# Twenty rows per ky in place of nineteen in the sampling products of a two-layer convolution kernel, with one x hat tile

## The chip, the cores and the metric

The kernel runs on one core of a Trainium2 chip. The metric is device time in microseconds, from the start to the end of one execution. TensorE is called PE here, VectorE DVE, ScalarE ACT, GpSimd POOL, and SyncE, which only issues DMAs, SP. All arithmetic is in fp32.

## What is computed

The input x holds 32 images of 128 channels and 32 by 32 pixels. Layer 0 adds to x a state space convolution over the 1024 pixels of the normalised image, 1024 channels wide, followed by a gated linear unit, a layer norm and a projection back to 128 channels. Layer 1 adds a deformable depthwise convolution of the normalised image. Its core is this loop over 64 taps (8 by 8), in which each tap samples the image at a shifted, fractional place:

```python
px = gx[None] + koff_t[0] + off_t[..., 0]
py = gy[None] + koff_t[1] + off_t[..., 1]
ix = px * sx - 0.5
iy = py * sy - 0.5
...
s = ((1 - dx) * (1 - dy))[:, None] * gather(y0i, x0i) + (dx * (1 - dy))[:, None] * gather(y0i, x0i + 1) + ((1 - dx) * dy)[:, None] * gather(y0i + 1, x0i) + (dx * dy)[:, None] * gather(y0i + 1, x0i + 1)
return (acc + s * w_t[None, :, None, None], None)
```

The offsets `off_t` come from a 3 by 3 depthwise convolution of the same image. They are small, so that all samples of one output row lie within a window of 8 by 8 pixels.

## The kernel before

`ssm_kernel_table` and `ssm_convolution` compute the state space convolution of all images and write it to HBM (`y_d`). They end near 1.5 ms and the change does not touch them. Then `main_block` does two things for each image, and interleaves them.

`first_part(b)` is the gated unit, norm and projection of image b. For each half image (512 pixels) and each of 8 groups of output channels it runs 8 matmuls for the gate (`gpg`, L808), 8 for the value (`gpv`, L831) and one for h (`gph`, L847), each 128 by 128 by 512. Between them DVE, ACT and POOL make the gate's sigmoid, the products, squares and sums. The result goes to `x1_d`.

`second_part(b)` is the deformable convolution of image b. It samples by matmul. An image column position u (0 to 38) is the output column plus the tap's kx, and v (1 to 37) is the output row plus the tap's ky. For each of 17 groups of u ("packs") there is a tile `ds` of 128 partitions by 16 slots by `CELLS` words. A slot is one (u, kx); its `CELLS` = 8 · `NV` words are 8 runs, one for each ky, of `NV` rows v. The partitions are two sides of 64: each side holds the weights of an 8 by 8 pixel window, and the sides divide the rows v. Side 0 starts at row `VBASE[0]`, side 1 at row `VBASE[1]`. Most packs have all 16 slots, two have 14, two 13 and one 8 (m in the code).

How a pack's `ds` comes about:

- `prepare(b)` computes the offsets of an image step by step during the second part of the image before. It lays them out by (u, ky, v): `spread` (L984) copies rows of `NV` words from HBM to HBM, `gather` (L999) loads them into a tile of 128 by `HSUB` words, and eight `hat` steps (L1010 and L1011 on ACT, L1012 the store from ACT's queue) make the weights in x, max(0, 1 − |offset − k|), for k = 0 to 7, each in a tile `dh` of the pool `hatpool`, and store them to HBM (`dhat`).
- `load_x` (L1110, on SP's queue) loads a pack's x weights from there into `ds`, and `load_y` (L1125) the plain offsets in y into `dhy`, in two halves.
- `hat_y` (L1145, L1146) makes the y weights of `dhy` on ACT in four parts, and `weights` (L1151) multiplies them into `ds` on DVE, in four parts per pack.

How it is used: a pack's rows are cut in four pieces (`blocks_of`). Piece 0 has the border rows, in runs of 6, 4, 2 and 1; pieces 1 to 3 have 4 rows each for all eight ky, and read them in two windows of 2 rows. The matmul (`dps`, L1227) has 64 rows of image pixels (`dxw`) as stationary operand, and as moving operand it reads `ds` at

```python
frm = s[half, 0, ky * NV + v0 - VBASE[side] + r0 :]
...
[CELLS, m],
[step * NV + skew, rows], [1, r1 - r0],
```

So a matmul of pieces 1 to 3 reads m slots times 8 ky times a pair of adjacent words. The two sides' matmuls are issued in turn. Pieces 0 and 1 form one block, pieces 2 and 3 another, and each piece and side has a PSUM bank, four in all. DVE multiplies what the block left in PSUM with the taps' weights into `prod` (L1243), which frees the banks; POOL adds up the eight ky (L1269) and adds to the accumulator (L1275). There are two `ds` tiles, three `dhy` tiles and, before the change, two `dh` tiles.

What sets the order: it is written out by hand. `run_along` takes pieces of `first_part(b + 2)` and `second_part(b)` in turn, so that both progress at the same share of a planned cost, and every engine has one queue in that order. The steps of `prepare(b + 1)` are issued at fixed places (`due`) in the second part of image b. In the opening, image 0 is prepared beside the first part of image 1; at the end, the second parts of the last two images run with nothing beside them.

Of the kernel before, what the change touches and what calls it, by code (L numbers as in the profile page):

```python
# [512 lines left out]


NU = W + 7
NV = 19
VBASE = (1, 19)
CELLS = 8 * NV
PIECES = 4
SIDE = NU * 8 * CELLS  # L520
# [69 lines left out]
def main_block(nc, tc, const, ins, x, u_d, y_d, x1_d, out, offmax):  # L590
# [18 lines left out]
    SB, HB = 2, 3  # L609
    KS = 16 * H  # L610
    ctx = ExitStack()
    with ctx:

        def pool(name, bufs, space=None):
            kw = {} if space is None else {"space": space}
            return ctx.enter_context(tc.tile_pool(name=name, bufs=bufs, **kw))

        one, two = pool("mb1", 1), pool("mb2", 2)
        spool, hypool, hatpool = pool("mbs", SB), pool("mbh", HB), pool("mbq", 2)
        ypool = pool("mby", YB)  # L620
        tpool = pool("mbt", 5)
        dram = pool("mb_dram", 2, DRAM)
# [84 lines left out]
        def at(t, offset, ap):  # L707
            return bass.AP(tensor=t.tensor, offset=t.offset + offset, ap=ap)
# [175 lines left out]
        def prepare(b):  # L884
# [97 lines left out]
            def spread(a, side):  # L982
                def run():
                    nc.sync.dma_start(  # L984
                        at(
                            rel_d[b % 2], a * NCOL + side * SIDE,
                            [[NV, 64], [8 * CELLS, NU], [1, NV]],
                        ),
                        at(
                            rel_n[b % 2], a * ASTEP + LEAST - 7 * H + VBASE[side],  # L990
                            [[KSTEP - 1, 64], [H, NU], [1, NV]],
                        ),
# [178 lines left out]
        def second_part(b, steps):  # L1171
# [6 lines left out]
            for n in range(NP):  # L1178
# [9 lines left out]
                for i in range(0, PIECES, 2):  # L1188
# [10 lines left out]
                    for piece in (i, i + 1):  # L1199
# [7 lines left out]
                        for parts in zip(blocks_of(0, piece), blocks_of(1, piece)):  # L1207
# [6 lines left out]
                            for part in range(len(parts[0][1])):  # L1214
                                for side in range(2):
                                    (ky, _, v0, _, step, skew), wins = parts[side]
                                    w, r0, r1 = wins[part]
                                    half = slice(64 * side, 64 * side + 64)
                                    frm = s[half, 0, ky * NV + v0 - VBASE[side] + r0 :]
                                    frm = bass.AP(  # L1220
                                        tensor=frm.tensor, offset=frm.offset,
                                        ap=[
                                            frm.ap[0], [CELLS, m],
                                            [step * NV + skew, rows], [1, r1 - r0],
                                        ],
# [139 lines left out]
@with_exitstack  # L1365
def kernel(ctx: ExitStack, tc: tile.TileContext, ins, out):
    nc = tc.nc
    x = ins["x"]
    cpool = ctx.enter_context(tc.tile_pool(name="const", bufs=1))
    dram = ctx.enter_context(tc.tile_pool(name="scratch", bufs=1, space=DRAM))  # L1370

    const = {}
    for name in ("gavg", "davg"):
        const[name] = cpool.tile([P, P], F32, tag=name, name=name)
        nc.sync.dma_start(const[name], ins[name])
    const["eps"] = cpool.tile([P, 1], F32, tag="eps", name="eps")
    nc.vector.memset(const["eps"], 1e-5)
    const["one"] = cpool.tile([P, 1], F32, tag="one", name="one")
    nc.vector.memset(const["one"], 1.0)
    offmax = cpool.tile([P, B], F32, tag="offmax", name="offmax")  # L1380

    kp_d = dram.tile([D, KPW], F32, tag="kp_d", name="kp_d")
    u_d = dram.tile([B, C, L], F32, tag="u_d", name="u_d")
    y_d = dram.tile([D, B, NJ, P], F32, tag="y_d", name="y_d")
    x1_d = dram.tile([B, C, L], F32, tag="x1_d", name="x1_d")

    ssm_kernel_table(nc, tc, ins, kp_d)
    ssm_convolution(nc, tc, const, ins, x, u_d, kp_d, y_d)
    main_block(nc, tc, const, ins, x, u_d, y_d, x1_d, out, offmax)
    deformable_redo(nc, tc, const, ins, x1_d, out, offmax)  # L1390
# [85 lines left out]
```

## Time and profile before

| | |
|---|---|
| Median of 3 runs | 12964.31 us (12957.98 to 12971.92) |
| The profiled execution | 13042.8 us, of which the span from the first to the last instruction is 13041.0 us |
| Busy in the span: PE, DVE, ACT, POOL | 12345.9, 8228.4, 5368.1, 8027.5 us |
| Sampling matmuls `dps`, L1227 | 23936 records, 2860.9 us busy |
| Weights `ds`, L1151 | 2176 instructions on DVE, mean 1317 ns |
| x hats, L1010 and L1011 | 256 each on ACT, 899 and 915 ns (median) |
| Opening of the deformable part, first `dps` | at 1849 us |

The profile is of one execution, and the other times are of executions without a profile. A row of the groups gives the line, engine and operation, what it writes and reads with the shape, the count, the busy time, the mean of one, and the engine's idle time just before with what ended it. PE's means overlap, because matmuls are pipelined: the distance between the starts of two records is what one costs.

### The profile page before, as it was taken

The numbers are of one execution on the slowest core, as the hardware profiler recorded it, in microseconds if no ns is written. First come the engines' busy times: TensorE is split into PE (matmuls) and PEld (weight loads), VectorE is DVE, ScalarE is ACT, GpSimd is POOL, SyncE is SP. The second block draws the span as 40 slices with busy tenths as digits, with TensorE's granted clock in tenths as the row PEclk, the third lists the DMA queues.
The fourth block names the chain that finished last, engine by engine and source line by source line (L and its number), as shares of the span: only waits on it lengthen the run. The fifth ranks groups of instructions, "written<-read, shape, count | busy, mean of one in ns | idle before, by whom it ended". The sixth has DMA issues, their size and how long they took to land.

```text
span 13041.0 us, 157419 instructions
## 1 busy us (share of the span) xinstructions
PE 12345.9 (95%) x51362; PEld 6725.6 (52%) x51362; DVE 8228.4 (63%) x14315; ACT 5368.1 (41%) x7823; POOL 8027.5 (62%) x6987
## 2 busy tenths in 40 slices
PE   7999999999999999999999999999999999999965
PEld 7999444444444444444444444444444444444444
DVE  5555136666666666666666666666666666666667
ACT  4443124444444444444444444444444444444443
POOL 2555126666666666666666666666666666666668
PEclk9999999999999999999999999999999999999976
DMA  7898146666676666666666676666666666676676
GB/s 237 268 278 275 49 101 169 171 169 165 176 173 171 166 166 163 178 169 169 172 165 171 169 176 167 170 166 164 174 174 166 174 165 171 170 171 174 163 174 176
DMA packets 1521916, 2276.56 MB, mean 175 GB/s; under 512 B 619586, under 2 KB 835266, under 8 KB 1520066
## 3 DMA queue, kind: packets, MB, share of 16 engines
q1 hardware_dynamic: 1382210, 1959.47, 60.7%
q10 hardware_dynamic: 89728, 172.65, 3.6%
q0 software_dynamic: 49152, 134.28, 3.4%
q8 instruction: 413, 6.77, 0.2%
q14 instruction: 413, 3.38, 0.1%
HBM read 1948.11 MB, written 400.64 MB: 180 GB/s over the span
## 4 chain that ended last, share of the span: by engine, by line
PE 85%; DMA 7%; SPq 3%; DVE 2%; issue 1%; ACT 1%; POOL 0%; ACTq 0%; DVEq 0%; POOLq 0%
PE gpv L831 26%; PE gpg L808 25%; PE dps L1227 18%; PE psy L320 5%; PE gpo L736 3%; PE psz L237 3%; PE gph L847 3%; DMA ds<-dhat 3%; DMA dhy<-rel_d 2%; DVE ds L1151 1%; SPq L1125 1%; SPq L984 1%; DVE prod L1243 1%; SPq L1110 1%; PE gpm L758 0%
## 5 line engine op out<-in xcount | busy, mean ns | idle before, releaser
L1269 POOL TENSOR_TENSOR prod<-prod 128x512 f32<-128x512 f32 (+3 forms) x3808 | 4939.0, 1329 | 1741.0 <-DVE prod L1243 1698.4
L1243 DVE TENSOR_TENSOR prod<-dps,k_weight_slots 128x512 f32<-128x512 f32 (+16 forms) x8704 | 3121.3, 406 | 1520.8 <-PE dps L1227 1327.5
L808 PE MATMUL gpg<-gy,g_w_glu 128*128 128x512 f32 x8192 | 3827.9, 610 | 130.8 <-DMA gy<-y_d 111.2
L831 PE MATMUL gpv<-gy,g_w_glu 128*128 128x512 f32 x8192 | 3743.1, 599 | 0.0
L1151 DVE TENSOR_TENSOR ds<-ds,dhy 128x608 f32<-128x608 f32 (+2 forms) x2176 | 2766.0, 1317 | 807.7 <-DMA ds<-dhat 563.6
L1227 PE MATMUL dps<-ds,dxw 64*128 64x128 f32 (+14 forms) x23936 | 2860.9, 383 | 417.3 <-DVE prod L1243 411.2
L1227 PEld LDWEIGHTS dps<-ds,dxw 64*128 64x128 f32 x23936 | 2015.6, 199 | 1553.6 <-DVE prod L1243 636.0
L808 PEld LDWEIGHTS gpg<-gy,g_w_glu 128*128 128x128 f32 x8192 | 1535.0, 193 | 2095.2 <-issue 1910.4
L831 PEld LDWEIGHTS gpv<-gy,g_w_glu 128*128 128x128 f32 x8192 | 1510.8, 190 | 1886.0 <-issue 1886.0
L869 POOL TENSOR_TENSOR gs<-gs,gq 128x512 f32<-128x512 f32 x448 | 642.8, 1435 | 2468.7 <-ACT gq L868 2468.7
L1145 ACT ACTIVATE dhy<-dhy,k_minus_y 128x608 f32<-128x608 f32 (+2 forms) x2176 | 1645.6, 756 | 795.8 <-DMA dhy<-rel_d 481.3
L1146 ACT ACTIVATE dhy<-dhy,one 128x608 f32<-128x608 f32 (+2 forms) x2176 | 1672.2, 768 | 70.7
L868 ACT ACTIVATE gq<-gr 128x512 f32<-128x512 f32 x448 | 280.7, 627 | 2514.4 <-DVE gr L860 2513.2
L839 DVE SCALAR_TENSOR_TENSOR gs<-gpv,k_b_glu,gs 128x512 f32<-128x512 f32 x512 | 383.9, 750 | 1430.9 <-PE gpv L831 1407.4
L815 ACT ACTIVATE gs<-gpg,k_b_glu 128x512 f32<-128x512 f32 x512 | 352.0, 688 | 1955.0 <-PE gpg L808 1938.5
L1275 POOL TENSOR_TENSOR dacc<-dacc,prod 128x256 f32<-128x256 f32 (+6 forms) x1184 | 1048.2, 885 | 92.8
L357 POOL DMA_DIRECT2D y_d<-yo x1024 | 590.0, 583 | 692.8 <-ACT yo L344 633.2
L320 PE MATMUL psy<-toe,z 128*128 128x192 f32 x4096 | 668.3, 326 | 7.6 <-DVE z L242 5.5
L320 PEld LDWEIGHTS psy<-toe,z 128*128 128x128 f32 x4096 | 663.4, 196 | 11.7 <-DVE z L242 6.8
L738 POOL TENSOR_TENSOR gs<-gs,gr 128x512 f32<-128x512 f32 x448 | 644.7, 1439 | 0.0
L335 DVE TENSOR_TENSOR psy<-psy,t 128x256 f32<-128x256 f32 (+2 forms) x768 | 333.8, 435 | 346.4 <-ACT t L328 329.6
L847 PE MATMUL gph<-gu,k_W_enc 128*128 128x512 f32 x1024 | 522.9, 592 | 0.0
(164 smaller groups left out, 6037.5 us busy)
## 6 DMA issues: line engine op xcount, KB each, us to landing
dhy<-rel_d SPq DMA_DIRECT2D x3264, 152.0 KB
ds<-dhat SPq DMA_DIRECT2D x832, 380.0 KB
ds<-dhat SPq DMA_DIRECT2D x448, 456.0 KB
dxw<-dxw_d SPq DMA_DIRECT2D x832, 224.0 KB
y_d<-yo POOLq DMA_DIRECT2D x1024, 128.0 KB, 4.2
gy<-y_d SPq DMA_DIRECT2D x512, 256.0 KB
u<-u_d SPq DMA_DIRECT2D x224, 512.0 KB
dhat<-dh ACTq DMA_DIRECT2D x256, 370.5 KB
```

Of the source, the lines that this page charges most:

```text
L320: nc.tensor.matmul(ps[:, c // 2, c % 2, :], rows[i][:, (g * CG + c0 + c) // 2, c % 2, :], toe[:, c0 + c, :], start=True, stop=True,)
L738: nc.gpsimd.tensor_add(sums[0], sums[0], r)
L808: nc.tensor.matmul(gate, w_glu[:, k, D + m * P : D + m * P + P], ys[k], start=(k == 0), stop=(k == KD - 1),)
L831: nc.tensor.matmul(val, w_glu[:, k, m * P : m * P + P], ys[k], start=(k == 0), stop=(k == KD - 1),)
L847: nc.tensor.matmul(h, w_enc[:, m * P : (m + 1) * P], u, start=True, stop=True)
L1145: nc.scalar.activation(t, t, AF.Abs, bias=minus_y)
L1146: nc.scalar.activation(t, t, AF.Relu, scale=-1.0, bias=const["one"])
L1151: nc.vector.tensor_mul(s_of[h][:, cut], s_of[h][:, cut], t)
L1227: nc.tensor.matmul(to[side][:, :, :, r0:r1], xw[half, w, :], frm, start=True, stop=True,)
L1243: nc.vector.tensor_mul(bass.AP(tensor=at_y.tensor, offset=at_y.offset, ap=[at_y.ap[0], [H, m], [step * (KS - 1) + skew, rows], [1, run],], ...
L1269: nc.gpsimd.tensor_add(row(to), row(to), row(frm))
L1275: nc.gpsimd.tensor_add(to, to, total[:, slot * H : (slot + nj) * H].rearrange("p (s y) -> p s y", y=H),)
```

## The change

`NV` becomes 20 and side 1 begins at row 18. So a run of one ky has 20 words, a slot 160 in place of 152, side 0 holds rows 1 to 20 and side 1 rows 18 to 37; the word at which a run begins, ky · NV + v0 − VBASE + r0, is even for every run of two or more words. `CELLS`, `SIDE`, `NCOL` and `HSUB` follow: a hat tile is 780 words wide in place of 741, a `ds` tile 2560 words in place of 2432. The pool of the hat tiles has one buffer in place of two. The number of instructions and DMAs and their order on each engine stay.

```diff
 NU = W + 7
-NV = 19
-VBASE = (1, 19)
+NV = 20
+VBASE = (1, 18)
 CELLS = 8 * NV
...
-        spool, hypool, hatpool = pool("mbs", SB), pool("mbh", HB), pool("mbq", 2)
+        spool, hypool, hatpool = pool("mbs", SB), pool("mbh", HB), pool("mbq", 1)
```

## The prediction

> **What bounds the kernel now.** I read the page first: which engine is busy, and for how long of the span.
>
> ```profile
> span 13041.0 us, 157419 instructions
> PE 12345.9 (95%) x51362; PEld 6725.6 (52%) x51362; DVE 8228.4 (63%) x14315; ACT 5368.1 (41%) x7823; POOL 8027.5 (62%) x6987
> ```
>
> Then the same split into stretches: the second is where 30 of the 32 images have both parts of the work side by side, the third is the end, where the deformable part (`second_part`) runs alone.
>
> ```profile
> 1850.00:12500.00 10650.00, 10362.79 (x40317) 5108.42 (x40314) 7015.96 (x12089) 4511.66 (x6179) 6945.60 (x5569) 0.98 0.68 169
> 12500.00:13041.00 541.00, 278.45 (x1515) 214.59 (x1514) 391.39 (x707) 224.22 (x298) 407.18 (x330) 0.63 0.71 179
> ```
>
> The order in a row is PE, PEld, DVE, ACT, POOL, clock, DMA share, GB/s. In the long stretch PE is busy 97%, DVE and POOL 66 and 65%. In the last it is busy half the time.
>
> Third, what PE still waits for, between 3000 and 12500 us:
>
> ```profile
> PE dps L1227 <- DVE prod L1243: 169.0, 53, 7.6
> PE gpg L808 <- DMA gy<-y_d: 87.5, 27, 5.6
> ```
>
> That is 257 us in 9500. So a nanosecond taken off PE's own stream in this stretch is worth nearly a nanosecond, as long as DVE follows.
>
> Last, how PE's time is made up, from the chain of waits and the groups by shape:
>
> ```profile
> 6004.55 3.43 PE gpg L808 x8
> 6018.48 2.38 PE dps L1227 x16
> L808 PE MATMUL gpg<-gy,g_w_glu 128*128 128x512 f32 x8192 | 3827.9, 610 | 130.8 <-DMA gy<-y_d 111.2 <-ACT gs L815 19.7
> L1227 PE MATMUL dps<-ds,dxw 64*128 64x256 f32 x9216 | 1562.5, 459 | 22.2 <-DVE prod L1243 18.0 <-ACT gn_r L914 3.4 <-ACT dvt L1032 0.7
> ```
>
> Each fp32 matmul leaves two records. The mean ns overlap, so I use pitches, the distance between starts. Eight 512-column records take 3.43 us: 429 ns each, 0.838 ns per column. The sampling block `dps` has 16 records of 256 columns. Its two sides, on partitions 0-63 and 64-127, start within 10 ns of each other, so this is eight pairs in 2.38 us. The start times of the single records give 273 ns from pair to pair inside the block, plus some 100 ns once at each end. At 0.838 ns a column, 256 columns would be 215 ns. **The sampling matmuls stream 27% slower per column than the GLU ones.** This gap is what the change is about.
>
> The records of different size (m slots, median pitch over the steady part) show where it comes from. Pair runs (rows read two words at a time): m=16: 274, 14: 242, 13: 225, 8: 139; that is 16.9 ns a slot, where 16 columns should take 13.4: 3.5 too much. The border piece's runs of six: 191, 167, 155, 12.0 a slot where 12 columns should take 10.1: 1.9 too much. Runs of four: 119, 105, 98, hardly too much. With 19 rows, a run begins at word 19·ky + constant, so half the pairs begin at an odd word and every fourth straddles a 16-byte line (two of eight ky). The line model: a slot's 8 pairs touch 10 lines; 16.9/10 is 1.7 ns a line. The odd run of six touches lines as 1+4+1, and 1.9 too much is again about two near-empty visits at 1.7 in place of two words at 0.84 (2·1.7 − 1.7). The odd run of four, 1+3, loses little, as seen.
>
> [...]
>
> **The change, part by part.**
>
> 1. *Even starts (PE, L1227).* With 20 rows ky·20 is even and a multiple of 4; starts become 6, 8 (side 0: v0=7, base 1) and 2, 4 (side 1: v0=20, base 18), the border runs 0, 42, 84 and 134, 94, 54. All even; no pair straddles a line, as the ds tiles begin on multiples of 32 bytes in both builds. The instruction order on PE is identical. New pitches: columns × 0.838 + 3.6 (the present fit's constant): m=16: 218, 14: 191, 13: 178, 8: 112 [...]. The line model gives the same for m=16: 128 lines × 1.7 = 218. Gain per pitch 56, 51, 47, 27 ns. Twelve pair pitches a pack (3 pieces × 2 windows × 2 records), packs per image 12, 2, 2, 1 of these sizes: 12·(12·56 + 2·51 + 2·47 + 27) = 10.7 us. Runs of six, two pitches a pack: 12·2·27 + 2·2·23 + 2·2·21 = 0.8. Runs of four, down to 111: 12·15 = 0.2. Together **11.8 us per image**, of a period of 355. On the path for 30 images: −353. Bounds: 60 ns a pitch if no constant stays (−380); nothing if reading is not the cause.
>
> 2. *Longer rows on DVE (L1151).* Four multiplies a pack grow by 5.3%: per image 54 of 608 to 640, 10 of 456 to 480, 4 of 304 to 320, 2032 elements. From the fastest 304 (460 ns) and 608 (773): 1.03 ns each, 2.1 us an image. DVE has a third of its time free: not on the path by itself.
>
> 3. *Longer rows on ACT.* Two activations of dhy per part: 0.84 ns an element (532 and 785 ns at 304 and 608), 3.4 us an image; hats 741 to 780, 16 × 33 ns = 0.5 us. ACT is 42% busy: nothing.
>
> 4. *More bytes.* ds and dhy loads, hats and rel all grow by 1/19. Issues times KB: ds 632, dhy 632, dhat 97, rel 36 MB, so +74 MB of 2277, DMA share .68 to about .72 with the shorter time. The number of issues on SP, ACT and POOL stays. A ds load comes out in the chain at 6 to 8 us, so each takes 0.3 to 0.4 us more. DVE already waits for them (451.6 us, 135 times in the steady part), and behind that wait in DVE's order stand the products that free PSUM for PE. The half pack in which they must land shrinks by 0.4 too. So DVE's ds are up to 0.8 us later per pack where they are late now, four or five packs an image, and a third of DVE's lateness reaches PE today (169 of 452). 5·0.8/3 is 1.3; I take 1.5 us an image: **+45**. Ends: 0, and 4 us an image (+120) if more packs turn late.
>
> 5. *One hat tile (L1010).* Each Abs now waits until the previous hat's store has left the tile; behind it on ACT stand sigmoids, squares and dhy. In steady images the next Abs comes 8.9 to 19 us after the previous issue (in the last set of hats 2 and 7 us, twice); its packets are gone after 4.5 us (median), 7.0 (nine in ten), 8.9 at most. Nothing, except single cases. In the opening (1787 to 1809 us) eight hats follow at 2.7 us each and the packets need 2.3 after issue: 1.9 + 2.3 = 4.2 us each, seven times 1.5, and PE is waiting for a sigmoid behind them (19.7 us in this place): **+10** (8 to 25).
>
> 6. *The end.* The last two images run alone; their chain is ds loads and ds multiplies, and PE at a lowered clock is too slow to be hurt by reading. 34 packs × (0.3 load, part of it hidden, + 0.13) : **+12** (0 to 25).
>
> Sum: −353 + 45 + 10 + 12 = **−286**. The profiled execution took 13042.8 us, its span 13041.0; that is 0.6% above the median 12964.31. 12757/13042.8 times the median: **12680**.
>
> **The rivals.**
>
> *Rival 1: half of it returns as DVE's lateness.* For: 20% of the packs' first blocks begin before the last products of the previous pack are done, and the median slack there is 1.6 us. Against: DVE's place is tied to PE's own results (gate, value and h groups in between), so it moves with PE. If each half pack loses 0.17 us of its 0.35, −150 net: about 12815.
>
> *Rival 2 (slower): PSUM writing, not reading, sets the pair pitch.* Place: L1227, where a window writes two of each four words. Price: pitch stays at 272-274, no gain; parts 4 to 6 cost about 1 us an image + 10 + 12, +52: 13016. Decides if pair pitches stay above some 268 ns (6 ns are worth what the costs are). Against: runs of six write without gaps and are slow too.
>
> *Rival 3: the hats stall ACT in every image.* From a landing later than the 8.9 us gap on: 2 us at each second hat, 8 us an image on ACT, perhaps half on PE: −353 + 120 + 67, about 12800. Packets' times speak against.
>
> *That the change doesn't act:* were the tile to begin at an odd word, all pairs would be odd; the addresses exclude it.
>
> **How the numbers follow.** Main case 0.70, rival 1 0.16, rival 2 0.09, rival 3 0.05. The main case's own ends are −380 + 8 = −372 (12594) and −353 + 120 + 25 + 25 = −183 (12782); reaching over rival 1 and 3 gives 12590 to 12840. A measurement can tell about 0.2%, 26 us. Faster: main, rivals 1 and 3 nearly whole, 0.88; same 0.03 (rival 2 with part of the gain); slower 0.09.
>
> **What would show it.** Right: L1227 64x256 mean from 459 to about 400 ns, x16 blocks of 1.95 us in the chain in place of 2.38, image period 346 us in place of 355, GLU records unchanged at 429. Wrong: blocks at 2.38 (rival 2); PE waits for prod L1243 or for gs far above 169 us (rivals 1, 3); ACT waits at L1010 for dhat in the hundreds of us.

## The result and the profile after

The changed kernel takes 12765.64 us in the median of 4 runs (12761.95 to 12769.27), against 12961.15 us before. The ratio is 0.9848, with a 95% interval of 0.9831 to 0.9865: 195.5 us faster, where 284 were forecast. The time lies in the stated range, and the direction is right. That is partly luck: two of the sum's terms were far off and partly made up for each other, as the steps below show.

The page after, and the same two stretches (the long one ends earlier because the kernel does; the order in a row is again PE, PEld, DVE, ACT, POOL, clock, DMA share, GB/s):

```profile
span 12767.5 us, 157327 instructions
PE 12216.4 (96%) x51362; PEld 6679.5 (52%) x51362; DVE 8277.2 (65%) x14315; ACT 5490.5 (43%) x7823; POOL 8094.1 (63%) x6987
...
q1 hardware_dynamic: 1382210, 2027.97, 60.4%
```

```profile
1850.00:12250.00 10400.00, 10253.61 (x40403) 5074.56 (x40402) 7085.27 (x12125) 4639.64 (x6196) 7028.63 (x5584) 0.99 0.68 180
12250.00:12767.00 517.00, 263.81 (x1442) 204.54 (x1439) 371.29 (x674) 217.83 (x282) 390.80 (x315) 0.63 0.72 192
```

PE was busy 97.3% of the long stretch and is now busy 98.6%. The DMA share stays at 0.68 although each image moves more bytes in less time (169 to 180 GB/s). That is the first surprise. The second is in PE's groups by shape (the rows of before stand in the prediction):

```profile
L808 PE MATMUL gpg<-gy,g_w_glu 128*128 128x512 f32 x8192 | 3771.8, 603 | 41.0 <-ACT gs L815 27.0 <-DMA gy<-y_d 14.0
L1227 PE MATMUL dps<-ds,dxw 64*128 64x256 f32 x9216 | 1533.4, 452 | 37.7 <-DVE prod L1243 34.1 <-ACT gn_r L914 2.9 <-ACT dvt L1032 0.7
```

The sampling matmul went from 459 to 452 ns where 400 was forecast; the wait of `gpg` for y loads fell from 111 to 14 us. By the start times of the records, the pair pitch at m=16 went from 274 to 267 ns, not to 218. The runs of six went from 191 to 163, as forecast (164).

The waits between 3000 and 12250 us tell where the rest went. First of before, then of after:

```profile
DVE ds L1151 <- DMA ds<-dhat: 436.5, 131, 13.7
ACT dhy L1145 <- DMA dhy<-rel_d: 252.7, 30, 11.9
PE dps L1227 <- DVE prod L1243: 163.4, 51, 7.6
PE gpg L808 <- DMA gy<-y_d: 84.9, 26, 5.6
```

```profile
DVE ds L1151 <- DMA ds<-dhat: 265.2, 135, 6.5
PE dps L1227 <- DVE prod L1243: 118.3, 80, 7.2
ACT dhy L1145 <- DMA dhy<-rel_d: 30.6, 26, 2.4
```

Waits for DMAs shrank, although each ds and dhy load is 5% longer. I cut every image into its 17 packs, by the start of each pack's first `dps`, and averaged over 27 images. The image period went from 354.9 to 345.8 us. Pack 8 alone went from 23.83 to 16.51 us, pack 9 from 23.99 to 23.23; packs 2 and 6 grew by 0.2 and 0.5, and most others lost 0.11 to 0.16 us each. So of 9.1 us, 7.3 are in one pack. It is the pack that begins while the spread (L984), issued in packs 6 and 7, is still running. Its rows of one ky were 76 bytes and are now 80. By the DMA packets, the four spreads of an image lasted 28.3 us from the first to the last packet and now last 21.0: the last packet came 5.4 us after pack 8's start and now comes 1.6 us before it. The 319488 row packets took 30.6 ns each in the mean and now take 20.1.

Here are packs 7 (from the first spread on) and 8 of one image, before and after:

```profile
7667.40:7691.97 24.57, 24.57 (x89) 11.44 (x88) 11.66 (x23) 8.58 (x15) 18.41 (x16) 1.00 1.11 88
7691.97:7717.36 25.39, 15.99 (x67) 7.54 (x66) 6.92 (x19) 3.62 (x5) 5.91 (x6) 0.83 1.08 181
```

```profile
7516.50:7541.09 24.59, 24.59 (x91) 11.58 (x89) 11.74 (x23) 8.96 (x15) 18.33 (x16) 1.00 0.90 113
7541.09:7556.20 15.11, 13.01 (x67) 6.78 (x66) 7.06 (x19) 3.84 (x5) 6.05 (x6) 1.00 1.04 274
```

During the spread the DMA engines are full (share 1.11, packets overlap) at 88 GB/s. The loads queued behind it come late, and in pack 8 PE is idle for 9.4 of 25.4 us. The chain that ended last shows the way before the change (pieces of it):

```profile
7673.14 7.50 SPq L984
7680.68 5.83 SPq L984
7686.61 6.09 SPq L1125
7692.74 9.21 DMA dhy<-rel_d
7702.01 5.40 DMA gy<-y_d
```

SP's queue is held while it issues the third and fourth spread: they took 7.6 and 5.0 us in the mean of 27 images, where an issue elsewhere takes about 0.6. The loads of dhy and gy stand behind them in the same queue. After the change the two take 6.0 and 3.7 us, and the chain of the same place goes through the loads alone, without L984:

```profile
7540.25 4.82 DMA dhy<-rel_d
7545.08 8.98 DMA ds<-dhat
```

Whether the held queue or the full engines delay the loads more was not separated.

While PE idles in pack 8, its granted clock falls: it is 1.00 in the mean from 7697 to 7702 us, 0.81 from 7702.8 to 7707 us, while PE waits 4.2 us for y loads, and 0.50 in the 5 us from 7707 us on, in which PE is busy throughout. The mean of pack 8's stretch is 0.83, and the same 67 records take 16.0 us of busy time in place of 13.0.

One caution: the profiled execution of before (13042.8 us) was 82 us above its median, the one after (12769.27) only 4. The traces differ by 273 us, the medians by 195, so what the two traces give for waits is up to 78 us too much. Two kernels below that were traced on one chip (the dense PSUM writes, with 19 and 20 rows, which leave PE's pitches as they are) give a fairer pair: the image period goes from 354.9 to 347.9 us, pack 8 from 23.6 to 17.9, a row packet from 30.7 to 22.0 ns. So pack 8 has 5.7 of 7.0 us. Below, each ratio is to the kernel before on the same chip as the experiment, whose median was between 13044 and 13071 us.

### The profile page after: what moved, and what is told of

It reads as the page before. It is cut to its first block, busy times and chain, and to the rows that moved or that the text cites. A ratio compares the mean times of both kernels' runs of the same rounds, so it can differ in the third digit from the quotient of the medians.

```text
span 12767.5 us, 157327 instructions
## 1 busy us (share of the span) xinstructions
PE 12216.4 (96%) x51362; PEld 6679.5 (52%) x51362; DVE 8277.2 (65%) x14315; ACT 5490.5 (43%) x7823; POOL 8094.1 (63%) x6987
## 2 busy tenths in 40 slices
DMA packets 1521915, 2350.16 MB, mean 184 GB/s; under 512 B 619586, under 2 KB 835266, under 8 KB 1520066
## 4 chain that ended last, share of the span: by engine, by line
PE 78%; DMA 7%; DVE 5%; POOL 3%; issue 2%; ACT 2%; SPq 2%; ACTq 0%; DVEq 0%; POOLq 0%
PE gpv L831 24%; PE gpg L808 23%; PE dps L1227 16%; PE psy L320 5%; PE psz L237 3%; DMA ds<-dhat 3%; PE gpo L736 3%; PE gph L847 3%; DVE ds L1151 2%; DVE prod L1243 2%; POOL prod L1269 1%; DMA dhy<-rel_d 1%; SPq L1125 1%; POOL do L1286 1%; DMA dxw<-dxw_d 1%
## 5 line engine op out<-in xcount | busy, mean ns | idle before, releaser
L1269 POOL TENSOR_TENSOR prod<-prod 128x512 f32<-128x512 f32 (+3 forms) x3808 | 4994.8, 1343 | 1614.0 <-DVE prod L1243 1571.4
L808 PE MATMUL gpg<-gy,g_w_glu 128*128 128x512 f32 x8192 | 3771.8, 603 | 41.0 <-ACT gs L815 27.0
L1151 DVE TENSOR_TENSOR ds<-ds,dhy 128x640 f32<-128x640 f32 (+2 forms) x2176 | 2821.2, 1342 | 620.7 <-DMA ds<-dhat 354.8
L1227 PE MATMUL dps<-ds,dxw 64*128 64x128 f32 (+14 forms) x23936 | 2778.3, 375 | 364.4 <-DVE prod L1243 329.5
L1227 PEld LDWEIGHTS dps<-ds,dxw 64*128 64x128 f32 x23936 | 1979.9, 197 | 1455.5 <-DVE prod L1243 560.5
L1145 ACT ACTIVATE dhy<-dhy,k_minus_y 128x640 f32<-128x640 f32 (+2 forms) x2176 | 1699.1, 781 | 532.5 <-DMA dhy<-rel_d 197.7
L1146 ACT ACTIVATE dhy<-dhy,one 128x640 f32<-128x640 f32 (+2 forms) x2176 | 1726.5, 793 | 71.1
```

The lines of the kernel that those rows point to most:

```text
L808: nc.tensor.matmul(gate, w_glu[:, k, D + m * P : D + m * P + P], ys[k], start=(k == 0), stop=(k == KD - 1),)
L1145: nc.scalar.activation(t, t, AF.Abs, bias=minus_y)
L1146: nc.scalar.activation(t, t, AF.Relu, scale=-1.0, bias=const["one"])
L1151: nc.vector.tensor_mul(s_of[h][:, cut], s_of[h][:, cut], t)
L1227: nc.tensor.matmul(to[side][:, :, :, r0:r1], xw[half, w, :], frm, start=True, stop=True,)
L1269: nc.gpsimd.tensor_add(row(to), row(to), row(frm))
```

## The experiments

Two theories stood against each other. **Rows theory**: the gain is the spread's rows in HBM. **Even-start theory**: it is PE's reading.

### One side odd, rows of 80 bytes

```diff
-VBASE = (1, 18)
+VBASE = (1, 19)
```

> Rows of 20 words and one hat tile as after the change, but the second side begins at row 19 again: every run of side 1 begins at an odd word, the HBM rows of 80 bytes stay. Rows theory (the gain comes from the 80 byte rows that the spread at L984 writes, 21 us an image in place of 28): spread 21 us, pack 8 at 16 to 17 us, total 12765 plus PE's own part, some 2 to 3 us an image: 12800 to 12870. Even-start theory (the gain comes from PE reading at even words): total back at 12960 or above, since now all runs of side 1 are odd and not half. For the pair pitch of PE at m=16 (274 before, 267 after): if a line of 16 bytes is the unit, the two windows differ (267 and 290 or more); if 8 bytes, both are alike, about 281.

Measured: ratio 1.0104 (1.0087 to 1.0121), slower than before. Both theories have a part. Pack 8 is at 16.4 us, as the rows theory says. But every ordinary pack is at 21.73 us, against 20.66 after the change and 20.80 before, because PE's blocks became longer:

```profile
6016.80 3.10 PE L1227 MATMUL dps<-ds,dxw 64*128 64x256 f32 x16
```

A block like this took 2.46 us before. By the single records, side 0 goes at 267 ns throughout. Side 1 goes at 267 in the window whose pairs are words 1 and 2 of a 16-byte line, and at 430 in the window whose pairs straddle two lines. That the boundary at multiples of 16 bytes counts was supposed in the prediction; here it is measured, 430 against 267 ns. 430 ns for 256 visited lines are 1.68 ns a line, or 1.67 with the 3.6 ns of the prediction's fit taken off. For an odd pair within a line nothing shows in this order of reading (267 and 267). Before, a quarter of the pairs straddled, at hops of 76 bytes, and the cost in the pitch was 7 ns. A quarter of the 163 ns here would be 41, so the price doesn't simply add up pair by pair.

### Rows of 19 words at a pitch of 20

```diff
-    rel_d[b % 2], a * NCOL + side * SIDE,
-    [[NV, 64], [8 * CELLS, NU], [1, NV]],
+    rel_d[b % 2], a * NCOL + side * SIDE + side,
+    [[NV, 64], [8 * CELLS, NU], [1, NV - 1]],
...
-    rel_n[b % 2], a * ASTEP + LEAST - 7 * H + VBASE[side],
+    rel_n[b % 2], a * ASTEP + LEAST - 7 * H + VBASE[side] + side,
```

The source rows are cut to 19 words too, and `rel_d` is filled with zeros once at the start.

> The changed kernel, but the spread writes rows of 19 words (76 bytes) at the pitch of 20; the word left out is read by no product. Rows theory, if the length of a row is what costs: spread 28 us again, pack 8 at 23 to 24 us, total 12900 to 12950. Rows theory, if packing at a pitch of 76 is what costs: spread 21 us, total 12765. Even-start theory: 12765 in any case.

Measured: ratio 0.9941 (0.9924 to 0.9957). The spread takes 27.1 us and pack 8 is at 22.3. PE's pitches are those of the changed kernel (267). The difference to the changed kernel's 0.9848 is 0.93%, some 120 us: the price of 76-byte rows at a pitch of 80. Some 8 us of it lie in the opening, where the first `dps` comes at 1866 us, against 1858 in the experiment before on the same chip. A row packet takes 25.2 ns in the mean, against 22.3 with the 80-byte rows of the experiment before and 32.0 with 76-byte rows packed (one hat tile, below), all on that chip. So a pitch of 80 alone doesn't bring the gain: it matters where a row begins and ends. This run can't tell the two apart, because side 1's rows here also begin 4 bytes later.

### The rows moved by one word

```diff
-    t = dram1.tile([2, NCOL], F32, ...
+    t = dram1.tile([2, NCOL + P], F32, ...
...
-    rel_d[b % 2], a * NCOL + side * SIDE,
+    rel_d[b % 2], 1 + a * NCOL + side * SIDE,
```

The gather and `load_y` read one word further on too.

> The changed kernel with the whole spread buffer in HBM moved by one word: rows of 80 bytes that begin at 4 beyond a multiple of 16. PE's reads are unchanged. If the row's place counts: spread 27 to 28 us as with 76 bytes, ratio to before 0.992 to 0.995. If its length counts: 21 us, ratio 0.985.

Measured: ratio 1.0039 (1.0024 to 1.0053). The place counts, more than I had expected: the spread takes 31.4 us with 80-byte rows that begin 4 bytes beyond a multiple of 16, a row packet 33.0 ns in the mean, and pack 8 is at 25.9. (On the same chip a kernel with unmoved rows, the slots inside each ky below, had 22.7 us and 21.9 ns.) One pack 8 and the waits:

```profile
7724.98:7749.73 24.75, 15.92 (x68) 7.48 (x67) 7.06 (x19) 3.72 (x5) 6.05 (x6) 0.86 0.95 199
```

```profile
DVE ds L1151 <- DMA ds<-dhat: 512.5, 153, 14.4
ACT dhy L1145 <- DMA dhy<-rel_d: 308.5, 29, 13.1
PE dps L1227 <- DVE prod L1243: 147.5, 77, 6.1
PE gpg L808 <- DMA gy<-y_d: 143.9, 26, 6.8
```

This kernel has the even starts and longer rows, and is slower than before. So the even starts do not carry the result alone. The move also shifts the reads of the gather and of `load_y`; the 2560-byte packets of `load_y` took 149 ns, against 145 in the unmoved kernel on that chip, a small part.

### No spread

```diff
             def spread(a, side):
                 def run():
+                    if b > 1:
+                        return
```

> The kernel before without the spread (L984) of images 2 to 31: they keep the offsets of the first two images. Rows theory: pack 8 falls from 23.8 to 15 or 16 us, DVE's wait for ds loads from 16.8 to under 8 us an image, total 12960 - 30 x 8 to 10 = 12660 to 12720. Even-start theory: the spread is hidden beside PE, total within 30 us of 12960.

From the third image on, this kernel leaves the spread out and keeps old offsets; nothing waits for a spread then. Measured: 0.9664 (0.9648 to 0.968), 442 us or 14.7 us an image, more than expected. Pack 8 is at 13.05 us and PE does not wait in it:

```profile
7489.52:7502.52 13.00, 13.00 (x68) 6.83 (x67) 8.16 (x22) 3.23 (x5) 6.47 (x6) 1.00 1.00 267
```

By the traces, the spread cost pack 8 10.8 us before the change and pack 9 another 3.0 (it is at 20.9 here); after it they still lose 3.5 and 2.3.

### Two attempts to move what is left

Spreads at steps 80, 88, 96 and 104 in place of 81 to 90, gather, hats and the last step (`ready`) later:

```diff
-    *((81 + 3 * i, spread(i // 2, i % 2)) for i in range(4)),
-    (99, gather), *((109 + 9 * k, hat(k)) for k in range(8)),
+    *((80 + 8 * i, spread(i // 2, i % 2)) for i in range(4)),
+    (113, gather), *((122 + 8 * k, hat(k)) for k in range(8)),
```

> The changed kernel with the four spreads issued 8 steps apart in place of 3 (80, 88, 96, 104), gather at 113, hats at 122 + 8k. Rows theory: pack 8 (16.5 us after the change, 13.1 with no spread) loses its bubble, packs 8 and 9 together 3 to 5 us an image: ratio to before 0.973 to 0.978. If the congestion is only moved to packs 6 to 9: 0.985.

Measured: 0.9833 (0.9817 to 0.985). Pack 8 is at 13.0, but pack 9 at 28.4 (23.2 after the change): the congestion moved, as the last two spreads are now issued after pack 8's start. The other attempt brings the offset steps closer together and the spread to steps 71 to 80:

```diff
-    *((44 + 3 * i, taps(i, i + 1)) for i in range(9)),
+    *((44 + 2 * i, taps(i, i + 1)) for i in range(9)),
...
-    *((81 + 3 * i, spread(i // 2, i % 2)) for i in range(4)),
+    *((71 + 3 * i, spread(i // 2, i % 2)) for i in range(4)),
```

> The changed kernel with the offset steps closer together, so that the four spreads are issued at steps 71 to 80 in place of 81 to 90 and are over when pack 8 loads the next half image's y; gather and hats stay. If the spread costs by standing before those loads: pack 8 falls from 16.5 to 13 to 14 us, pack 9 stays, ratio to before 0.974 to 0.980. If it is only moved into packs 6 and 7: 0.985.

Measured: 0.9814 (0.9797 to 0.983). In its trace pack 8 is still at 16.5 and the image period 346.0, as in the changed kernel's trace; packs 5 and 7 grew by 1.1 and 0.6 us and pack 6 shrank by 2.0. What the ratio shows beyond 0.9848 is unexplained, and the changed kernel itself was not run on that chip. The spread's last packet now comes 7.1 us before pack 8 and yet the pack stays. Why is open: the y loads of the next half image are issued in it, but so they are in the kernel without a spread and in the one with the spreads apart, where it is at 13.0.

### One hat tile in the kernel before

```diff
-hatpool = pool("mbq", 2)
+hatpool = pool("mbq", 1)
```

> The kernel before with one x hat tile. Both theories: the hat stores have left the tile before the next Abs in all but the opening, so +10 us (8 to 25): 12960 to 12985. If the single tile costs in every image: 13000 or more.

Measured: 1.0008 (1.0001 to 1.0015), 1 to 20 us where 10 were forecast. In the changed kernel's trace, what ACT waited for before the hats' Abs is

```profile
  DMA dr<-rel_d: 344.6, 32
  DMA dhat<-dh: 19.5, 9
```

The second line is the new wait: 9 of 256.

### The write to PSUM without gaps

```diff
-    nc.tensor.matmul(
-        to[side][:, :, :, r0:r1],
+    dst = to[side][:, :, :, r0:r1]
+    if (r1 - r0) < run:
+        n2 = (hi - lo) // 2
+        dst = ps[side][:, lo + part * n2 : lo + (part + 1) * n2].rearrange(...)
+    nc.tensor.matmul(
+        dst,
```

> The changed kernel, with each window of pieces 1 to 3 written to its own half of the PSUM bank without gaps. DVE still reads the bank in the old order, so the rows that these pieces' products belong to are changed; the count and size of all instructions stay. Even reads are in it. If the gaps in the PSUM write set the pair pitch (267 ns at m=16 after the change): 215 to 220, PE's blocks of 16 records at 1.95 us, 10 us an image: ratio to before about 0.960 to 0.968. If hopping between pairs in the read sets it: pitch stays 267, ratio 0.985.

> The kernel before with the same dense PSUM write (and the same changed order of rows). It shows what odd starts cost when the write has no gaps: by 1.667 ns for each 16 byte line visited (the all-crossing window of side 1 with base 19 took 430 ns for 256 visits), 160 visits are 267 to 270 ns. If the read has no line limit: 215 to 220.

Measured: 0.9846 (0.9829 to 0.9862), with pitch 267; with 19 rows, 274 and 13044.99 us in one run. In these two kernels DVE still reads the old order, so their rows are exchanged; the instructions are the same. Gaps of two words in the PSUM write cost nothing here, and rival 2's mechanism is out. A third kernel reads the two halves in the right order on DVE, with a fourth dimension in the code's access pattern (the instruction's record shows three, merged):

> The changed kernel with the dense PSUM write, and DVE's product reading the two halves in the right order through a fourth dimension. If the write sets the pair pitch, 215 to 220 ns and a ratio of 0.960 to 0.970 as long as DVE's products (686 ns at 128x512) stay under 800 ns; if DVE's reading of pairs with hops costs it 300 ns more each, 6 a pack, DVE gains 1.8 us a pack and half of PE's gain is lost: 0.975. If the read sets the pitch: 0.985.

Measured: 0.984 (0.9823 to 0.9856). The pitch is 267 again, and DVE's product stays at 687 ns at 128x512.

### The slots inside each ky

So the gaps in the write don't make the 267 ns. This experiment keeps all pairs and changes the order in which a matmul goes through them, in the read and, with it, in the write:

```diff
-            frm.ap[0], [CELLS, m],
-            [step * NV + skew, rows], [1, r1 - r0],
...
+    if piece > 0:
...
+            ap=[frm.ap[0], [NV, rows], [CELLS, m], [1, 2]],
...
+        dst = dst.rearrange("p s k v -> p k s v")
```

> The changed kernel, but a matmul of pieces 1 to 3 goes through the 16 slots inside each ky: from pair to pair it hops 640 bytes (40 lines of 16) in place of 80 (5 lines). If the hop's size sets the 267 ns for 128 even pairs (2.08 ns a pair, where two words stream in 1.67): another pitch, 215 to 220 at best or well over 267. If it is the price of any pair on its own line: 267 again.

Measured: 12625.89 us in one run, against 13043.75 before on that chip, 0.968. The pitch is 220 ns at m=16, 194 at 14 and 180 at 13, which are the forecast's numbers for the change (218, 191, 178) within 3 ns. Ordinary packs are at 20.11 us in place of 20.66. It beats both kernels by far more than runs differ. The write now hops from pair to pair too, and PE is faster: so it was the read that held the pitch at 267. The same order in the kernel before:

> The kernel before (19 rows, half the pairs odd, two hat tiles) with the slots inside each ky in the matmuls of pieces 1 to 3, as in e10. If even starts pay once the small hop is gone: 1.667 ns for each of 160 visited lines, 267 to 275 ns at m=16, no gain, ratio 1.000. If the small hop was all that there was: 220 ns as in e10, 9 to 10 us an image, ratio 0.978 to 0.985, and pack 8 stays at 23 us or more.

Measured: 1.019 (1.0173 to 1.0207), slower than before, pitch 334 ns; neither of the two expected cases. The groups and blocks of both, first with 20 rows, then with 19:

```profile
L1235 PE MATMUL dps<-ds,dxw 64*128 64x256 f32 x9216 | 1336.1, 407 | 54.4 <-DVE prod L1250 49.8 <-ACT gn_r L914 2.9 <-ACT dvt L1032 0.7
...
6009.93 2.03 PE L1235 MATMUL dps<-ds,dxw 64*128 64x256 f32 x16
```

```profile
L1235 PE MATMUL dps<-ds,dxw 64*128 64x256 f32 x9216 | 1795.1, 520 | 5.8 <-ACT gn_r L914 2.7 <-DVE prod L1250 2.4 <-ACT dvt L1032 0.7
...
6010.01 2.93 PE L1235 MATMUL dps<-ds,dxw 64*128 64x256 f32 x16
```

In this order the 20 rows (even starts, and hops of 640 in place of 608 bytes) are worth 114 ns a pitch; in the order that the change keeps, 7. Pair pitches at m=16, all measured:

| order of reading | starts | ns |
|---|---|---|
| ky inside (hop of 76 bytes) | half odd | 274 |
| ky inside (80 bytes) | even | 267 |
| ky inside (80 bytes) | odd, words 1 and 2 of a line | 267 |
| ky inside (80 bytes) | all straddling two lines | 430 |
| slots inside (640 bytes) | even | 220 |
| slots inside (608 bytes) | half odd | 334 |

A price per visited line explains the fourth row, and the first roughly. It explains neither the 267 of pairs 80 bytes apart nor the 334: 128 and 160 lines at 1.68 would be 215 and 269. The cause of these two stays open; no experiment separated hop length from the place of the next pair.

## Why the prediction was right or wrong

**Part 1, even starts: the term that failed.** It said 11.8 us an image. Measured block lengths (medians at m=16) went from 2.57 + 2.39 to 2.48 + 2.33 us a pack, 0.14 us, or 2.4 us an image: a fifth. Within it the runs of six were right (28 ns gained a pitch, 27 forecast). The pairs were wrong (7 in place of 56). The step that failed is the line model, "16.9/10 is 1.7 ns a line", and with it "128 lines × 1.7 = 218": those 128 lines took 267 ns, 2.1 a line. It had two numbers to explain, 16.9 and 12.0 ns a slot, and I took the whole excess of the pairs for straddling. Most of it is the price of pairs in this order, which the change keeps. My estimate of 1.7 ns a line is the time of two words at 0.838 ns, so that even pairs, two words to a line, were to lose next to nothing against 215 ns for 256 columns; they take 267. The stated sign, "blocks of 1.95 us", did not come; it came with the slots inside (1.96 us). Another, "image period 346 us", did come, for the reason of part 4. The border's runs of 6 gave no evidence on pairs.

**Part 4, more bytes: wrong in sign, and the second step that failed.** It said +45 us, and put what the new row length does to the spread at nothing. The added bytes are as worked out (2276.56 to 2350.16 MB), but I asked how much longer the loads become, and not what else the row length touches. The page counts 619586 packets under 512 B, and 319488 of them are the spread's; the trace had its 28 us an image. "The number of issues stays" is true, yet each of 2496 rows in each spread became cheaper by a third in the mean. With even reads held the same, the rows' place and length are worth 0.93% (19 words) to 1.9% (moved by a word) of the time.

**Parts 2 and 3.** The fastest ds multiply went from 773 to 809 ns at the full part, 36 as against 33; dhy from 787 to 814 in the median, 27 as forecast. PE, busy 98.6% of the long stretch, leaves little room for either on the path.

**Part 5, the hat tile.** Right, as far as 1 to 20 us can tell. The opening's first `dps` came 3.6 us later in the trace.

**Part 6, the end.** From the start of image 30 to the end it was 534.9 us and is 535.7: nothing, where +12 was forecast. That reading does not hurt PE at a lowered clock can be seen in both traces: where the granted clock was 0.5, the median pair pitch at m=16 was 427 ns before (69 pitches) and is 427 after (50), twice 213.5, where 256 columns at 0.838 ns are 215.

**The rivals.** Rival 2 had its own test, a pitch that stays above some 268 ns. The measured 267 all but met it, and yet its mechanism fell: dense PSUM writes changed nothing. It gave 13016 us; what made the kernel faster all the same was none of the cases I had listed. Rivals 1 and 3 did not occur: PE's wait for the products fell, and the hats wait 9 times.

**The sum.** Even reads with 76-byte rows in the pitch of 20 give 0.9941, about −77 us; the rows of 80 bytes at multiples of 16 give the other −120. So the reason that the forecast gave, worth 353 us in its sum, brought some 77 us, costs included. The larger part came from a buffer that the sum had only counted as bytes, and that the total came out in the stated range was luck.

## What to carry to other kernels

When a size changes, follow it through every buffer that it lays out, the HBM copies with it: whether a row had 76 or 80 bytes was worth more here (some 120 us) than the reads the change was about (some 77). When a model of a rate is fitted to a trace, ask which other order of the same accesses would give another rate; the 20 rows brought much on PE (114 ns a pitch, not 7) only once the order of reading was changed too. A stall of 10 us in one pack of 17 is found by cutting the trace into periods, not by the averages of a stretch. The chain then tells what stands in the queue ahead of the late load.

## What the runs showed of the hardware that I had not expected

- HBM rows of 80 bytes written at multiples of 16 bytes took 20.1 to 22.3 ns a packet in the mean of a kernel; at 4 bytes beyond, 33.0 (21.9 unmoved on that chip); 76-byte rows packed, 30.2 to 32.0. The median is 12 ns before the change as after it, at means of 30.6 and 20.1: it is the tail of slow packets that differs. The runs do not show why the place counts.
- With hops of 640 bytes PE took 220 ns for 256 columns of even pairs, close to the 215 that 0.838 ns a column gives (the rate of the 512-column records, 429 ns each; an fp32 matmul leaves two records, 8192 for the 4096 of `gpg`), and with hops of 80 it took 21% more (267). At both hops each pair is on a 16-byte line of its own, so a new line for every pair is not what makes the difference.
- Two-word gaps in PE's writes to PSUM cost nothing measurable (267 and 267, 274 and 274, where reading sets the pitch), and with the slots inside each ky, where every pair is written with a hop, the pitch still came down to 220.
